# One of six GpSimd products per job goes to VectorE in two scan layers of a four-layer stack

## The chip, the cores and the metric

The kernel runs on one core of a Trainium2 chip, in one launch. The metric is device time in microseconds (us), the median of three runs. A core has five engines with queues of their own: TensorE (PE; its weight loads appear as PEld), VectorE (DVE), ScalarE (ACT), GpSimd (POOL) and SyncE (SP), which here issues nearly all transfers (DMA). An engine works off its queue strictly in order, and waits for others through semaphores.

## The reference, cut to what matters

The input x is eight images of 192 channels and 56 x 56 pixels, in float32. Four layers follow, each `x = x + layer(group_norm(x))`. Layer 0 is an involution. Layers 1, 2 and 3 are Mamba blocks: projections, a causal convolution over four positions, silu, and a selective scan along the 3136 pixels. The scan is what the change touches:

```
dbl = xc @ xproj.T                    # dt's low rank part, B and C, 16 states each
dt  = softplus(dbl[dt] @ dtproj.T + bias)
h   = h * exp(dt * A) + (dt * xc) * B     # for each of 16 states and each inner channel
y   = sum over states of h * C
out = ((y + xc * D) * silu(z)) @ out_w.T
```

Layer 1 runs three mambas of 512 inner channels on slices of 64 channels; layers 2 and 3 run one each with 384 inner channels.

## The kernel before

**Chunks and jobs.** An image is cut into 7 chunks of T = 448 pixels, so a layer has 56 chunks. A job is one mamba on one chunk: 168 jobs in layer 1, 56 in layer 2 and 56 in layer 3. The inner channels of a job come in nd groups of 128 (nd = 4 in layer 1, 3 in layers 2 and 3).

**Units.** The 16 states of a group are taken in q = 0 to 3 quarters. A unit is one group and one quarter: 32 channels x 4 states on the 128 partitions, four rows r of 448 pixels each, 1792 elements per partition. A job has nd x 4 units, so 12 in layers 2 and 3, numbered m = 0 to 11 with q = m % 4. A unit passes these stages:

- `inputs_begin` (L737): ScalarE copies the carried state into the tile uhg (9 buffers).
- the product (dt * xc) * B into uhg. Two engines can make it. GpSimd (`inputs_by_pool`, L748) reads B from `rows[0, q]`, an SBUF tile that a transfer has spread over the partitions (`row_in`, L629, rows<-bc). VectorE (`inputs_by_vector`, L754) reads B from a PSUM bank, b, which TensorE has filled by a small matmul (`spread_b`, L723). There is one such bank.
- `decays` (L729): ScalarE writes exp(dt * A) into one of two PSUM banks, da, two rows in each.
- `scan` (L758): VectorE runs the recurrence, two scans per unit, h = 0 and h = 1, each over one da bank.
- `keep` (L762): ScalarE copies the last column out as carry.
- `readout` (L767): GpSimd multiplies by C.
- `reduce` (L776): TensorE sums the states into the bank y; at q = 0 it first puts xc * D there (L773). After the last quarter of a group `gated` (L792) multiplies with silu(z) on VectorE.

**The order of the work** is written out by hand in the loop over the units (L847 and on). At step k, with m = k % 12, it issues in this order: gated, if q = 3; reduce(k-3); the first half of the background steps; scan(k, 0); decays(k+1, 0); inputs_begin(k+3); inputs_by_pool(k+2); readout(k-2); inputs_by_vector(k+1); spread_b(k+2); the second half of the background steps; scan(k, 1); keep(k); decays(k+1, 1). The set `pool_units` (L699) says which units GpSimd multiplies; spread_b and inputs_by_vector leave these out, inputs_by_pool leaves out the others. `pool_rows` is the set of q that occur in it: only for these is the row of B transferred, at m = 8 + q of the job before. So a product by GpSimd is issued two steps ahead of its scan, and one by VectorE one step ahead, between the two scans of the unit before.

**The background** is the next job's preparation, planned into two places per step (`places`, with the stretches of `bounds`): convolutions up to m = 3; at m = 4 the silu block, in which ScalarE changes its table, makes silu of xc and of z (L596, L577) and changes back (L569), then the output projection of the job before (L1129, added by L1135 on VectorE) and x_proj (L601, evicted by L605 and L606); at m = 5 and 6 the remainder of B (L612, L613, evicted by L617) and the deltas (L635, evicted by L640); at m = 7 the softplus block (L643); then the products dt * xc (L650), the stores (ops<-dt), the loads of the operands (rep<-ops, L713) and the gates. All background matmuls share two PSUM banks, mm: a third one waits until ScalarE or VectorE has evicted the first. `nothing` (L782) issues matmuls that add zero. In layer 2 a chunk also ends with batch-norm statistics on VectorE (L298), and every seventh chunk with the group norm of a whole image.

Of the kernel before, what the change touches and what calls it, by code (L numbers as in the profile page):

```python
# [86 lines left out]
def conv_mamba_stack(ctx: ExitStack, tc: tile.TileContext, a, out):  # L87
# [604 lines left out]
    def ssm_layer(pool, w, jobs, n_slots):  # L692


        nd = w.nd
        units = [(i, j, q) for i in range(len(jobs)) for j in range(nd) for q in range(NQ)]
        groups = [(i, j) for i in range(len(jobs)) for j in range(nd)]
        per_job = nd * NQ
        pool_units = {1, 3, 5, 7, 9, 11, 13, 15} if nd == 4 else {1, 3, 6, 7, 9, 11}  # L699
        pool_rows = sorted({m % NQ for m in pool_units})  # L700
        us = [Layer() for _ in jobs]
        carry = []
# [449 lines left out]
    for layer, w in enumerate((w1, w2, w3), 1):  # L1152
        with ExitStack() as stack:
            scan_banks(stack)
            pool = stack.enter_context(tc.tile_pool(name=f"ssm{layer}", bufs=1))
            load_weights(pool, w)
            with tc.manual_schedule():
                if layer == 1:
                    ssm_layer(pool, w, mamba_jobs(pool, w), 3)
                else:  # L1160
                    ssm_layer(pool, w, dense_jobs(pool, w, layer), 1)
# [69 lines left out]
```

## Time and profile before

| what | before |
|---|---|
| median of three runs | 25285.75 us (25262.34 to 25312.53) |
| the profiled execution: time, span | 25314.83 us, 25313.0 us |
| mean granted TensorE clock | 0.827 of full speed |
| layer 2, from its first matmul L1082 to that of layer 3 | 17417 to 21390 us |
| layer 3, to the end of the span | 21390 to 25313 us |
| scans L758 (VectorE) | 8064 x 2011 ns |
| readouts L767 (GpSimd) | 4032 x 3675 ns |
| products by GpSimd, L748 | 2016 x 3987 ns |
| products by VectorE, L754 | 2016 x 2000 ns |
| rows of B spread by TensorE, L723 | 2016 x 406 ns |

The durations of neighbours on one engine overlap by some hundredths of a microsecond in the profile, so a sum goes better by the distance from one start to the next: 1.92 to 1.95 us for a scan, 3.65 for a readout, 3.96 for a product by GpSimd, 1.91 to 1.93 for one by VectorE. In a line of the timeline the first two numbers are the start in us from the span's beginning and the duration in us (of all, where "x3" says that three were merged); in brackets stands how long the engine was idle before it, and what released it. In a row of the table by stretch each engine has its busy time and its number of instructions; behind them come the granted clock, the share of the DMA engines and GB/s.

### The profile page before, as it was taken

To read this page: it belongs to the slowest core of one execution; us is meant where nothing else is said; L and a number is where in the kernel's file an instruction comes from. 1 tells how busy PE (TensorE), PEld (TensorE's weight loads), DVE (VectorE), ACT (ScalarE), POOL (GpSimd) and SP (SyncE) were. 2 spreads that over 40 slices of the span, in tenths; PEclk is the share of its full clock that TensorE was granted. 3 is DMA by queue.
4 is the path that set the end of the run, shared out by engine and by line. 5 is a ranking of instruction groups with operands and counts; after the bars stand their busy time and mean duration, and the time that the engine had idled before them with its cause. 6 is when DMAs were issued, how large, how long until landed. Compare 5 with 4: busy or idle time off the path is not lost.

```text
span 25313.0 us, 232064 instructions
## 1 busy us (share of the span) xinstructions
PE 21123.4 (83%) x71870; PEld 6720.0 (27%) x71870; DVE 22641.3 (89%) x15661; ACT 16946.5 (67%) x32354; POOL 23383.1 (92%) x6772
## 2 busy tenths in 40 slices
PE   9988888888888888888888888888888887888888
PEld 3322222222222222222222222222333332333332
DVE  8879988998899889998998899897999998999998
ACT  1137776767766776766776676676777776777776
POOL 4469999999999999999999999998999998999999
PEclk9988777877777777777777787778888888888888
DMA  4433333333333333333333333333444443444443
GB/s 106 105 101 123 122 119 117 122 121 119 118 122 121 119 120 119 123 119 119 123 119 120 121 120 118 121 119 108 139 141 136 139 140 120 141 138 139 138 145 128
DMA packets 1184872, 3132.61 MB, mean 124 GB/s; under 512 B 163756, under 2 KB 446404, under 8 KB 1183496
## 3 DMA queue, kind: packets, MB, share of 16 engines
q1 hardware_dynamic: 1180824, 3116.70, 37.9%
q8 instruction: 564, 9.24, 0.1%
q14 instruction: 684, 5.60, 0.1%
q10 hardware_dynamic: 2800, 1.06, 0.0%
HBM read 2399.92 MB, written 555.55 MB: 117 GB/s over the span
## 4 chain that ended last, share of the span: by engine, by line
DVE 29%; PE 25%; ACT 19%; issue 11%; POOL 9%; DMA 6%; SPq 2%; DVEq 0%; POOLq 0%; ACTq 0%
DVE uhg L758 20%; ACT da L729 8%; DVE uhg L754 6%; POOL uhg L767 6%; PE y L776 4%; PE mm L635 4%; POOL uhg L748 3%; PE mm L416 3%; DMA rows<-bc 3%; PE y L782 2%; ACT L569 2%; PE y_inv L451 2%; PE y L773 2%; PE mm L612 2%; DMA rep<-ops 2%
## 5 line engine op out<-in xcount | busy, mean ns | idle before, releaser
L758 DVE TENSOR_TENSOR_SCAN uhg<-da,uhg 128x898 f32<-128x898 f32 x8064 | 15928.1, 2011 | 1284.0 <-ACT da L729 1261.9
L767 POOL TENSOR_TENSOR uhg<-uhg,rows 128x1792 f32<-128x1792 f32 x4032 | 14746.3, 3675 | 654.5 <-ACT carry L762 425.9
L729 ACT ACTIVATE da<-rep,k 128x448 f32<-128x448 f32 x16128 | 10255.9, 636 | 1816.6 <-DVE uhg L758 1438.7
L748 POOL TENSOR_TENSOR uhg<-rep,rows 128x1792 f32<-128x1792 f32 x2016 | 8038.2, 3987 | 375.5 <-DMA rep<-ops 206.2
L776 PE MATMUL y<-uhg,k 128*32 128x448 f32 x32256 | 4756.8, 666 | 562.0 <-POOL uhg L767 560.2
L754 DVE TENSOR_TENSOR uhg<-rep,b 128x1792 f32<-128x1792 f32 x2016 | 4031.8, 2000 | 658.9 <-PE b L723 615.1
L762 ACT COPY carry<-uhg 128x4 f32<-128x4 f32 x4032 | 787.3, 195 | 3514.0 <-DVE uhg L758 3464.3
L773 PE MATMUL y<-xc,w_d 128*128 128x448 f32 x2016 | 1522.0, 850 | 1580.5 <-DVE zs L792 1580.3
L782 PE MATMUL y<-w_d,k 128*128 128x448 f32 (+1 forms) x5166 | 2465.1, 586 | 0.0
L1026 PE MATMUL mm<-xs,k 128*128 128x448 f32 x2688 | 1289.7, 617 | 479.6 <-DMA xs<-xg 318.7
L776 PEld LDWEIGHTS y<-uhg,k 128*32 128x32 f32 x32256 | 695.1, 117 | 3664.1 <-issue 2204.0
L1082 PE MATMUL mm<-v,w_in 96*128 96x448 f32 x2688 | 1427.9, 662 | 199.7 <-ACT zs L676 92.4
L635 PE MATMUL mm<-dbl,w_dt 36*128 36x448 f32 (+1 forms) x2016 | 1469.0, 840 | 127.0 <-ACT k L617 127.0
L782 PEld LDWEIGHTS y<-w_d,k 128*128 128x128 f32 x5166 | 1035.4, 215 | 1486.5 <-issue 1459.8
L436 POOL TENSOR_TENSOR x<-x,one 96x448 f32<-96x448 f32 x560 | 633.3, 1135 | 668.3 <-DVE one L428 650.7
L612 PE MATMUL mm<-dbl,k 16*16 16x448 f32 x1120 | 692.7, 707 | 515.7 <-ACT dbl L605 515.7
L428 DVE TENSOR_TENSOR prod<-mm,shifted 128x448 f32<-128x448 f32 x1680 | 932.6, 609 | 207.8 <-PE mm L416 187.3
L1109 PE MATMUL mm<-xin,w_conv 128*128 128x448 f32 x2688 | 1076.4, 543 | 2.0 <-ACT xin L674 1.0
L773 PEld LDWEIGHTS y<-xc,w_d 128*128 128x128 f32 x2016 | 455.0, 265 | 2191.9 <-DVE zs L792 1509.5
L647 PE MATMUL mm<-xc,k 128*128 128x448 f32 x2016 | 983.7, 599 | 31.1 <-DVE dt L650 30.3
L723 PE MATMUL b<-k,k 96*128 96x448 bf16 x2016 | 819.1, 406 | 129.9 <-DVE uhg L754 129.8
L593 ACT ACTIVATE xc<-mm,k 128x448 f32<-128x448 f32 x1008 | 615.3, 627 | 438.9 <-PE mm L1026 327.1
(134 smaller groups left out, 19720.0 us busy)
## 6 DMA issues: line engine op xcount, KB each, us to landing
rep<-ops SPq DMA_DIRECT2D x4032, 448.0 KB, 5.7
ops<-dt SPq DMA_DIRECT2D x1008, 448.0 KB, 3.3
rows<-bc SPq DMA_DIRECT2D x1792, 224.0 KB, 6.2
shifted<-xpad SPq DMA_DIRECT2D x672, 179.0 KB, 4.6
xg<-stream SPq DMA_DIRECT2D x168, 336.0 KB, 3.7
xr<-stream SPq DMA_DIRECT2D x168, 336.0 KB, 5.3
stream<-xr SPq DMA_DIRECT2D x112, 336.0 KB, 3.2
xs<-xg SPq DMA_DIRECT2D x224, 112.0 KB, 6.1
```

The lines of the kernel that those rows point to most:

```text
L612: nc.tensor.matmul(u.left[m][:NS, :T], lhsT=ident[:NS, :NS], rhs=u.dbl[:NS, :], start=True, stop=False)
L635: nc.tensor.matmul(u.dps[j][:, :T], lhsT=w.dtw[:, j * 128 : (j + 1) * 128], rhs=u.dbl[:nk, :], start=True, stop=True)
L729: nc.scalar.activation(t[:, 64 + 449 * r : 512 + 449 * r], reps[k // NQ][:, 2 * h + r, 0, :], AF.Exp, scale=w.neg_a[:, j * NR + 2 * h + r, ...
L748: nc.gpsimd.tensor_mul(uhg[k][:, :, 1:], reps[k // NQ][:, :, 1, :], b)
L754: nc.vector.tensor_mul(uhg[k][:, :, 1:], reps[k // NQ][:, :, 1, :], b)
L758: nc.vector.tensor_tensor_scan(v, banks.da[h][:, 63:961], v, 0.0, ALU.mult, ALU.add)
L767: nc.gpsimd.tensor_mul(v, v, us[i].rows[1, q].unsqueeze(1).to_broadcast([128, NR, T]))
L773: nc.tensor.matmul(ys[k // NQ][:, :T], lhsT=w.dd[:, j, :], rhs=us[i].xc[:, j, :], start=True, stop=False)
L776: nc.tensor.matmul(y[32 * r : 32 * r + 32, :T], lhsT=fold, rhs=uhg[k][:, r, 1:], start=False, stop=(q == NQ - 1))
L782: nc.tensor.matmul(ys[k // NQ][:, : nd * 112], lhsT=zeros, rhs=w.dd.rearrange("p j e -> p (j e)")[:, : nd * 112], start=False, stop=False,)
L1026: nc.tensor.matmul(pm[:, :T], lhsT=w.inconv[:, k, j * 128 : (j + 1) * 128], rhs=ck.xs[:, i, 2 - 2 * k : 2 - 2 * k + T], start=(k == 0), st ...
L1082: nc.tensor.matmul(pm[:, :T], lhsT=w.inw[:, k, m * 128 : (m + 1) * 128], rhs=ck.v[:, k, :], start=(k == 0), stop=(k == NCT - 1),)
```

## The change

For jobs of 12 units, which are those of layers 2 and 3, unit 6 leaves the set of GpSimd's units:

```diff
-        pool_units = {1, 3, 5, 7, 9, 11, 13, 15} if nd == 4 else {1, 3, 6, 7, 9, 11}
+        pool_units = {1, 3, 5, 7, 9, 11, 13, 15} if nd == 4 else {1, 3, 7, 9, 11}
```

In a job VectorE's products were those of units 0, 2, 4, 5, 8 and 10; unit 6 joins them, so that 4, 5 and 6 stand in a row. Its product is no longer issued on GpSimd's queue at step 4 but on VectorE's at step 5, between the two scans of unit 5; spread_b is issued for it at step 4. `pool_rows` becomes {1, 3} instead of {1, 2, 3}, so the transfer of the row of B for q = 2 at m = 10 falls away. The tile tag of these rows keeps its four buffers. Layers 0 and 1 are issued as before.

## The prediction

> **What bounds the kernel now.** I read the busy line of the page first, then the table by stretch over the steady parts of layers 2 and 3 (the only ones whose set of units changes), and then the timelines of single jobs.
>
> ```profile
> PE 21123.4 (83%) x71870; PEld 6720.0 (27%) x71870; DVE 22641.3 (89%) x15661; ACT 16946.5 (67%) x32354; POOL 23383.1 (92%) x6772
> ```
> ```profile
> 17600.00:21300.00 3700.00, 3138.96 (x11083) 1130.85 (x11083) 3412.05 (x2176) 2736.07 (x5215) 3576.50 (x964) 0.89 0.42 138
> 21600.00:25250.00 3650.00, 3192.75 (x11025) 1128.75 (x11024) 3320.54 (x2016) 2708.14 (x5186) 3572.55 (x963) 0.88 0.42 140
> ```
>
> The columns are PE, PEld, DVE, ACT, POOL, then the granted clock. GpSimd is busy 97% and 98% of these stretches, VectorE 92% and 91%. That looks like a GpSimd bound, but the jobs speak against it. I took the distance from the first scan of a job to the first scan of the next. In layer 2 it is 68.24 us in 38 of 55 cases, within 0.02 us; seven are 75 to 79 (the end of an image, with its group norm) and nine average 70.1; the mean is 69.6. In those equal jobs GpSimd's idle time varies from 0 to 6.2 us and the readout of unit 0 trails its scan by 1.5 to 8.7 us, yet the period does not move. So GpSimd does not set it. VectorE's idle hardly varies, 4.8 to 5.0 us a job, always in the same four places: ahead of the first scans of units 1, 5, 7 and 8 (1.33, 1.72, 1.01, 0.89), each ended by ScalarE's decays. Layer 2 goes by a ring of VectorE and ScalarE. The part that matters, on VectorE, from the second scan of unit 4 to the first of unit 7:
>
> ```profile
> 18743.63 2.02 DVE L758 TENSOR_TENSOR_SCAN uhg<-da,uhg 128x898 f32<-128x898 f32 x1
> 18745.57 0.59 DVE L1135 TENSOR_TENSOR xr<-xr,mm 96x448 f32<-96x448 f32 x1
> 18747.88 2.03 DVE L758 TENSOR_TENSOR_SCAN uhg<-da,uhg 128x898 f32<-128x898 f32 x1 [1.72 <-ACT da L729]
> 18749.83 0.59 DVE L1135 TENSOR_TENSOR xr<-xr,mm 96x448 f32<-96x448 f32 x1
> 18750.34 5.85 DVE L758 TENSOR_TENSOR_SCAN uhg<-da,uhg 128x898 f32<-128x898 f32 x3
> 18756.11 0.59 DVE L792 TENSOR_TENSOR zs<-zs,y 128x448 f32<-128x448 f32 x1
> 18757.71 2.03 DVE L758 TENSOR_TENSOR_SCAN uhg<-da,uhg 128x898 f32<-128x898 f32 x1 [1.01 <-ACT da L729]
> ```
>
> and on ScalarE, from the carry of unit 5 to the decays of unit 7, with TensorE's two groups between:
>
> ```profile
> 18752.39 0.20 ACT L762 COPY carry<-uhg 128x4 f32<-128x4 f32 x1 [0.17 <-DVE uhg L758]
> 18752.49 1.30 ACT L729 ACTIVATE da<-rep,k 128x448 f32<-128x448 f32 x2
> 18753.82 0.52 ACT L617 CAST k<-mm 16x448 bf16<-16x448 f32 x1
> 18754.36 0.64 ACT L640 ACTIVATE dt<-mm,k 128x448 f32<-128x448 f32 x1
> 18755.77 0.63 ACT L640 ACTIVATE dt<-mm,k 128x448 f32<-128x448 f32 x1 [0.78 <-PE mm L635]
> 18756.31 1.30 ACT L729 ACTIVATE da<-rep,k 128x448 f32<-128x448 f32 x2
> ```
> ```profile
> 18753.83 0.96 PE L776 MATMUL y<-uhg,k 128*32 128x448 f32 x8
> 18754.72 1.02 PE L635 MATMUL mm<-dbl,w_dt 44*128 44x448 f32 x2
> ```
>
> Read it as a chain: the second scan of unit 5 ends (18752.28), ScalarE's carry, the second decays of unit 6, the eviction L617, which frees one of the two mm banks for TensorE's L635, then L640, then the first decays of unit 7, then VectorE may scan. VectorE's own way (two scans, L792) is 1.01 us shorter.
>
> Layer 3 has no batch-norm statistics. Twelve of its 55 distances are 67.0 to 67.1 us, with the same four waits; that is its undisturbed period, 67.02. But the mean is 68.78: 17 are 68.36, and 25 average 69.9. In nearly all of the long ones a stretch of half clock lies on the deltas: in one at 23415 to 23425 the granted clock is 0.50, L635 x2 takes 1.86 instead of 1.02, and the wait ahead of unit 7 is 2.76 instead of 1.01. In the 68.36 jobs a short slow stretch lies on the convolutions. In layer 2's equal jobs the slow stretch always falls some 54 to 68 us into the job, where it costs nothing.
>
> **The change part by part.** Per job, in 112 jobs.
>
> GpSimd loses one L748: 3.96 us from its start to the next instruction's. A job needs 12 x 3.65 + 6 x 3.96 = 67.6 us of GpSimd, then 63.6. Layer 2 shows what that is worth: nothing, since a changing lag leaves the period alone. The one place where GpSimd does end the work is the drain of each layer, five readouts in a row; the last scan of layer 3 ends at 25294.2 and the last readout at 25301.3. There GpSimd comes up to 3.96 earlier while VectorE's scans come up to 1.93 later: I take 2 us gained per layer, 4 in all (bounds 0 and 8).
>
> SP loses one row transfer per job (rows<-bc, 224 KB), since no unit with remainder 2 is left with GpSimd. GpSimd's first product of a job already waits for such a transfer (70.5 us in 36 waits in the layer 2 stretch) without moving the period: 0, from 0 to a little gained.
>
> TensorE gains one L723 of 0.35 us. It must wait until VectorE has read the row of unit 5 out of the only b bank, which ends at 18743.7, and it stands ahead of the output projection (L1129, begun at 18743.01). So L1129, L601 and L605 move by about 1.1 us. L1129's first half then ends near 18746.5, and the addition L1135 ahead of unit 5's scan still fits into its 1.72 us of idle. L601 would end near 18751.2, when ScalarE comes to L605 (18751.27). Cost 0. The cover is thin: at half clock, up to about 1 us in such a job.
>
> VectorE gains one L754, 1.93 us from start to next start. In program order it stands after the first scan of unit 5 and ahead of L1135 and of that unit's second scan. All that follows begins 1.93 later: the second scan, hence carry, decays of unit 6 and L617. The 1.01 us of idle ahead of unit 7 does not hide it, because the idle ends at the end of a chain that begins at this very scan. One thing is given back: L617 ended about 18754.3, but TensorE was in L776 until 18754.7 and only then began L635. With L617 at about 18756.2 TensorE is free, so L635 starts about 0.3 sooner after it. Shift: 1.93 - 0.28 = 1.65 us per job. Bounds: 0, if all four waits could hide it, and 1.93.
>
> The dearest unknown is TensorE's clock, since the job's length and TensorE's pauses both change. Before, its price is 1.76 us a job in layer 3 (68.78 - 67.02) and about 0 in the equal jobs of layer 2. For each layer after it I bound the price by 0 and 1.76. For layer 2 I keep what there is. For layer 3, whose new undisturbed period of 68.67 comes near layer 2's old one, I take half, 0.88.
>
> What sets a slow stretch off can be seen once: TensorE waits for a readout, and the clock is low after it.
>
> ```profile
> 18773.71 1.72 PE L776 MATMUL y<-uhg,k 128*32 128x448 f32 x8 [4.05 <-POOL uhg L767]
> ```
> ```profile
> 18772.00:18786.00 14.00, 10.17 (x25) 3.08 (x26) 14.00 (x9) 7.47 (x16) 12.75 (x4) 0.53 0.70 255
> ```
>
> [...]
>
> [...]
>
> **The sum.** Layer 2: 56 x 1.65 = 92. Layer 3: 56 x (1.65 - 0.88) = 43. Drains: -4. Together 131 us on the profiled 25314.83. That execution is 0.1% above the median of the runs shown, 25285.75; I add the 131 to the median: **25417 us**.
>
> **The rivals.**
> 1. The clock gets worse: with periods off 68.24 layer 2 loses its harmless slot and pays 1.76, layer 3 keeps its 1.76. 92 + 92 + 99 - 4 = 279: 25565. For it: layer 3's scatter. Against: a longer job leaves TensorE more room.
> 2. The product is partly hidden, say a shift of 0.8 us, as much as the smallest of the four waits: 112 x 0.8 - 56 x 0.88 - 4 = 36: 25322, no change to be told.
> 3. Faster: GpSimd is the bound after all, and layer 3's scatter and layer 2's nine jobs of 70.1 come from its lag through TensorE's readout sums (L776 waits for L767, 645 us in PE and PEld together in layer 3's stretch). Then 56 x 1.76 + 9 x 1.86 = 115 go, and with the product lying in the waits around units 5 and 7 the time is 25286 - 115 - 4 = 25167. It turns to the slow side from a shift of 119/112 = 1.06 us per job. Against: 1.01 is all the idle there, and it moves with the scan.
> 4. The edit does nothing at run time: 25286. The sets of units feed spread_b, both input functions and the row loads alike, so I hardly believe it.
>
> **How the numbers follow.** Forecast 0.58, clock worse 0.18, partly hidden 0.16, faster 0.06, nothing 0.02. The forecast's own range is 82 to 180 (layer 3's clock price 0 or whole): 25368 to 25466. The range of 8 in 10 takes in the partly hidden case and most of the worse clock: 25315 to 25540. A measurement here can tell about 0.2%, 51 us. Slower by more: 0.58 + 0.18 = 0.76; within: 0.18; faster: 0.06.
>
> **What the profile after would show.** L748 1904 times and L754 2128 times. VectorE's scans of units 5 and 6 no longer three in a row after L1135, but a product ahead of it. The equal period of layer 2 at 69.9, the wait ahead of unit 7 near 0.7, the others unmoved; GpSimd 89 to 92% busy in both stretches, with its added idle ahead of a readout or a row transfer. I am wrong if layer 2's commonest period is below 69.3 (the chain does not begin at unit 5's scan), or if layer 3's least period falls below 67.0 (then GpSimd did bind it).

## The result, and the profile after

The changed kernel takes **25569.79 us** (median of four runs, 25557.68 to 25585.67), against 25287.67 for the kernel before in the same runs (25262.34 to 25312.53): a ratio of 1.0112, 95% interval [1.0094, 1.0129]. It is slower, as forecast, but by 282 us in place of 131, and outside the range. The time is that of rival 1, though only in part by the way that rival 1 gave.

The page after, busy times first, then the two groups of products:

```profile
PE 21286.5 (83%) x71982; PEld 6758.0 (26%) x71982; DVE 22861.9 (89%) x15773; ACT 16949.1 (66%) x32354; POOL 22947.4 (90%) x6660
...
L748 POOL TENSOR_TENSOR uhg<-rep,rows 128x1792 f32<-128x1792 f32 x1904 | 7590.8, 3987 | 724.1 <-DMA rows<-bc 477.1
L754 DVE TENSOR_TENSOR uhg<-rep,b 128x1792 f32<-128x1792 f32 x2128 | 4253.4, 1999 | 676.7 <-PE b L723 633.9
```

The counts are as forecast (1904 and 2128): 112 products went over. GpSimd has 436 us less to do and nothing came of it. The table by stretch over the steady parts of layers 2 and 3 (PE, PEld, DVE, ACT, POOL, granted clock):

```profile
17600.00:21300.00 3700.00, 3138.74 (x10650) 1109.37 (x10646) 3352.19 (x2132) 2618.62 (x4981) 3220.21 (x871) 0.85 0.39 129
21700.00:25350.00 3650.00, 3132.89 (x10739) 1105.35 (x10736) 3322.97 (x2005) 2623.28 (x5023) 3257.96 (x881) 0.86 0.40 132
```

GpSimd went from 97 and 98% to 87 and 89% (89 to 92 was forecast). VectorE has one product more per job and is not busier: 91% in both. So the jobs grew by more than the product. And the granted clock fell from 0.89 and 0.88 to 0.85 and 0.86.

The time by jobs (distance from the first scan of a job to the next, 55 distances per layer):

| | before | after | grown by |
|---|---|---|---|
| layer 2, mean; commonest; least | 69.59; 68.24; 68.23 | 72.81; 72.03; 71.38 | 177 us in 55 |
| layer 3, mean; commonest; least | 68.78; 68.36; 67.01 | 71.04; 70.79; 69.76 | 124 us in 55 |

Layers 0 and 1 are the same in both. The first matmul of layer 2 comes 22 us earlier after (17394.7 against 17416.8), which is scatter: over the fourteen kernels of this document the first scan of layer 2 starts anywhere from 17431 to 17468. So the whole of it lies in the two layers, spread over all jobs. VectorE from the end of the second scan of unit 4 on, in a job with the commonest distance (the 32nd of layer 2, begun at 19705.97):

```profile
19733.75 0.62 DVE L1135 TENSOR_TENSOR xr<-xr,mm 96x448 f32<-96x448 f32 x1 [0.76 <-PE mm L1129]
19735.22 2.03 DVE L758 TENSOR_TENSOR_SCAN uhg<-da,uhg 128x898 f32<-128x898 f32 x1 [0.85 <-ACT da L729]
19737.17 1.99 DVE L754 TENSOR_TENSOR uhg<-rep,b 128x1792 f32<-128x1792 f32 x1
19739.08 0.61 DVE L1135 TENSOR_TENSOR xr<-xr,mm 96x448 f32<-96x448 f32 x1
19739.61 5.85 DVE L758 TENSOR_TENSOR_SCAN uhg<-da,uhg 128x898 f32<-128x898 f32 x3
19745.38 0.59 DVE L792 TENSOR_TENSOR zs<-zs,y 128x448 f32<-128x448 f32 x1
19747.50 2.03 DVE L758 TENSOR_TENSOR_SCAN uhg<-da,uhg 128x898 f32<-128x898 f32 x1 [1.52 <-ACT da L729]
19749.90 2.02 DVE L754 TENSOR_TENSOR uhg<-rep,b 128x1792 f32<-128x1792 f32 x1 [0.38 <-PE b L723]
```

The new L754 stands where the forecast put it. Before unit 5 the wait for L1129 (0.76) has taken the place of half of the old 1.72: the late output projection is hidden, as forecast. But the wait ahead of unit 7 is 1.52, where 0.7 was forecast, and the product of unit 8 now waits 0.38 for its row of B, which it did not before. ScalarE and TensorE in the same job:

```profile
19741.66 0.20 ACT L762 COPY carry<-uhg 128x4 f32<-128x4 f32 x1 [2.11 <-DVE uhg L758]
19741.76 1.30 ACT L729 ACTIVATE da<-rep,k 128x448 f32<-128x448 f32 x2
19743.09 0.52 ACT L617 CAST k<-mm 16x448 bf16<-16x448 f32 x1
```
```profile
19739.83 0.91 PE L612 MATMUL mm<-dbl,k 16*16 16x448 f32 x2 [0.59 <-DVE xr L1135]
...
19740.86 1.02 PE L635 MATMUL mm<-dbl,w_dt 44*128 44x448 f32 x2
19741.81 0.96 PE L776 MATMUL y<-uhg,k 128*32 128x448 f32 x8
19743.67 1.86 PE L635 MATMUL mm<-dbl,w_dt 44*128 44x448 f32 x2 [0.90 <-ACT k L617]
19745.45 1.67 PE L612 MATMUL mm<-dbl,k 16*16 16x448 f32 x2
```

Carry and L617 are late by the new product. TensorE, which before went from L776 straight into L635, now pauses 0.90 for the bank; in layer 2 it does so 53 times, 43.6 us in all. (The 0.59 ahead of the first L612 is not new: in the prediction's job TensorE waited 0.81 there, for L605.) Behind the pause the same L635 takes 1.86 instead of 1.02 and L612 1.67 instead of 0.91: **half clock**. The table by stretch, cut at like parts of a job, shows it. First the kernel before, in the job of the prediction's timelines, then the one after (the granted clock stands behind the five engines):

```profile
18754.62:18765.62 11.00, 9.83 (x41) 3.37 (x38) 9.11 (x8) 10.02 (x18) 11.00 (x4) 1.00 0.07 26
18765.62:18772.62 7.00, 4.03 (x18) 1.55 (x16) 7.00 (x6) 4.01 (x9) 7.00 (x3) 1.00 0.68 194
18772.62:18786.86 14.24, 11.03 (x27) 3.44 (x28) 14.24 (x9) 7.47 (x16) 12.99 (x5) 0.52 0.71 253
```
```profile
19741.97:19752.97 11.00, 10.10 (x27) 2.09 (x19) 9.10 (x6) 8.14 (x15) 7.53 (x3) 0.54 0.00 1
19752.97:19765.97 13.00, 11.24 (x51) 4.51 (x48) 11.46 (x11) 9.12 (x17) 12.15 (x4) 1.00 0.61 205
19765.97:19778.00 12.03, 6.01 (x16) 1.95 (x16) 12.03 (x9) 6.08 (x13) 9.05 (x3) 0.57 0.55 204
```

Before, the only slow stretch of this job lay at its end, where VectorE was busy throughout (14.24 of 14.24), so it cost nothing. After, a second one lies 36 to 47 us into the job, on the deltas and the matmuls behind them, whose results VectorE waits for. What that does to VectorE over the whole of layer 2 (busy, mean ns, then idle ahead of the group), before and after:

```profile
L758 DVE TENSOR_TENSOR_SCAN uhg<-da,uhg 128x898 f32<-128x898 f32 x1344 | 2663.6, 2012 | 276.2 <-ACT da L729 271.3 <-POOL uhg L767 4.4 <-DVE uhg L754 0.5
L754 DVE TENSOR_TENSOR uhg<-rep,b 128x1792 f32<-128x1792 f32 x335 | 668.6, 1996 | 8.2 <-PE b L723 8.2
L650 DVE TENSOR_TENSOR dt<-dt,mm 128x448 f32<-128x448 f32 x165 | 95.4, 603 | 4.0 <-PE mm L647 3.6 <-ACT dt L643 0.2
L1135 DVE TENSOR_TENSOR xr<-xr,mm 96x448 f32<-96x448 f32 x110 | 65.1, 593 | 0.0
```
```profile
L758 DVE TENSOR_TENSOR_SCAN uhg<-da,uhg 128x898 f32<-128x898 f32 x1344 | 2663.0, 2011 | 246.3 <-ACT da L729 243.1 <-POOL uhg L767 2.6 <-DVE uhg L754 0.5
L754 DVE TENSOR_TENSOR uhg<-rep,b 128x1792 f32<-128x1792 f32 x391 | 781.7, 1999 | 39.9 <-PE b L723 39.9
L650 DVE TENSOR_TENSOR dt<-dt,mm 128x448 f32<-128x448 f32 x165 | 100.4, 612 | 29.5 <-PE mm L647 23.6 <-ACT dt L643 3.1
L1135 DVE TENSOR_TENSOR xr<-xr,mm 96x448 f32<-96x448 f32 x110 | 67.4, 613 | 41.1 <-PE mm L1129 41.1
```

The products cost 113 us more (56 of 2.0). Of the scans' idle only 30 us went, although the product covers about 1 us ahead of unit 5 in each job, since part came back ahead of unit 7. And 98 us of new waits for TensorE stand in three places (31.7, 25.5 and 41.1).

### The profile page after: what moved, and what is told of

Its sections match the earlier page's. It is cut to its first block, busy times and chain, and to the rows that moved or that the text cites. A ratio compares the mean times of both kernels' runs of the same rounds, so it can differ in the third digit from the quotient of the medians.

```text
span 25583.5 us, 231744 instructions
## 1 busy us (share of the span) xinstructions
PE 21286.5 (83%) x71982; PEld 6758.0 (26%) x71982; DVE 22861.9 (89%) x15773; ACT 16949.1 (66%) x32354; POOL 22947.4 (90%) x6660
## 4 chain that ended last, share of the span: by engine, by line
DVE 32%; PE 26%; ACT 20%; issue 10%; DMA 5%; POOL 5%; SPq 1%; DVEq 0%; POOLq 0%; ACTq 0%
DVE uhg L758 22%; ACT da L729 8%; DVE uhg L754 7%; PE mm L635 5%; PE y L776 4%; POOL uhg L767 3%; PE mm L416 3%; DMA rows<-bc 2%; PE y L782 2%; ACT L569 2%; PE mm L612 2%; PE y L773 2%; PE y_inv L451 2%; POOL uhg L748 2%; ACT zs L577 2%
## 5 line engine op out<-in xcount | busy, mean ns | idle before, releaser
L767 POOL TENSOR_TENSOR uhg<-uhg,rows 128x1792 f32<-128x1792 f32 x4032 | 14745.2, 3674 | 1012.7 <-ACT carry L762 788.6
L748 POOL TENSOR_TENSOR uhg<-rep,rows 128x1792 f32<-128x1792 f32 x1904 | 7590.8, 3987 | 724.1 <-DMA rows<-bc 477.1
L754 DVE TENSOR_TENSOR uhg<-rep,b 128x1792 f32<-128x1792 f32 x2128 | 4253.4, 1999 | 676.7 <-PE b L723 633.9
L776 PE MATMUL y<-uhg,k 128*32 128x448 f32 x32256 | 4753.0, 665 | 68.0 <-POOL uhg L767 66.1
L773 PE MATMUL y<-xc,w_d 128*128 128x448 f32 x2016 | 1582.5, 882 | 1992.6 <-DVE zs L792 1992.4
L635 PE MATMUL mm<-dbl,w_dt 36*128 36x448 f32 (+1 forms) x2016 | 1575.6, 896 | 207.2 <-ACT k L617 206.3
L776 PEld LDWEIGHTS y<-uhg,k 128*32 128x32 f32 x32256 | 695.4, 117 | 3209.2 <-issue 2360.6
L1082 PE MATMUL mm<-v,w_in 96*128 96x448 f32 x2688 | 1321.7, 619 | 204.0 <-ACT zs L676 98.2
L773 PEld LDWEIGHTS y<-xc,w_d 128*128 128x128 f32 x2016 | 472.8, 274 | 2674.5 <-DVE zs L792 1986.6
L612 PE MATMUL mm<-dbl,k 16*16 16x448 f32 x1120 | 744.8, 756 | 503.5 <-ACT dbl L605 459.8
```

What stands on the lines that cost most here:

```text
L612: nc.tensor.matmul(u.left[m][:NS, :T], lhsT=ident[:NS, :NS], rhs=u.dbl[:NS, :], start=True, stop=False)
L635: nc.tensor.matmul(u.dps[j][:, :T], lhsT=w.dtw[:, j * 128 : (j + 1) * 128], rhs=u.dbl[:nk, :], start=True, stop=True)
L748: nc.gpsimd.tensor_mul(uhg[k][:, :, 1:], reps[k // NQ][:, :, 1, :], b)
L754: nc.vector.tensor_mul(uhg[k][:, :, 1:], reps[k // NQ][:, :, 1, :], b)
L767: nc.gpsimd.tensor_mul(v, v, us[i].rows[1, q].unsqueeze(1).to_broadcast([128, NR, T]))
L773: nc.tensor.matmul(ys[k // NQ][:, :T], lhsT=w.dd[:, j, :], rhs=us[i].xc[:, j, :], start=True, stop=False)
```

## The experiments

**The theories.** (A) The new product delays carry and L617; TensorE, which at that point has only small matmuls, pauses for the bank; its clock goes to half on the deltas, and this doubles the price. (B) The price is VectorE's longer work, the product plus waits that follow from it, and the clock only goes along with the longer job. (C) It comes from GpSimd's changed load, or from the row transfer that fell away. (D) It is the single b bank, which delays L1129, a cover that I had called thin.

The measure that separates them is read from the clock records of each trace. In those of the two kernels TensorE's clock is full or half, and it changes after whole multiples of 3.413 us (1657 of 1658 stretches before, 1825 of 1826 after); such a length is called a slot below. The measure is how many of the 12 us from 36 to 48 us of a job are at half clock, on average over the 55 jobs that have a distance. Beside it stand the start of L617 in layer 2's jobs (the second of the three in a job; median, from the job's first scan), the mean distances of layers 2 and 3, and the time against the kernel before, which was timed beside each group of experiments (medians 25304.45 beside e1 to e4, 25290.9 beside e5 to e8, 25306.21 beside e9 to e12).

| kernel | L617 at | half clock, 36 to 48: layer 2; 3 | mean distance: layer 2; 3 | us, ratio to before, interval |
|---|---|---|---|---|
| before | 35.2 | 0.9; 4.6 | 69.59; 68.78 | |
| after | 37.1 | 9.5; 9.4 | 72.81; 71.04 | 25569.79, 1.0112 [1.0094, 1.0129] |
| e1 after, 3 zero groups | 38.4 | 1.1; 0.7 | 72.02; 70.18 | 25485.37, 1.0075 [1.0063, 1.0088] |
| e2 after, product earlier | 35.3 | 1.9; 3.1 | 69.59; 68.30 | 25266.81, 0.9984 [0.9975, 0.9993] |
| e3 unit 7 in place of 6 | 35.2 | 3.2; 4.1 | 69.55; 68.36 | 25254.19, 0.9983 [0.9975, 0.9992] |
| e4 before, less GpSimd | 35.2 | 0.7; 2.7 | 69.13; 68.53 | 25274.73, 0.9988 [0.9979, 0.9997] |
| e5 after, L617 first | 35.0 | 5.0; 3.7 | 70.57; 69.10 | 25363.83, 1.0027 [1.0018, 1.0036] |
| e6 after, 3 weak groups | 38.4 | 10.0; 9.9 | 74.69; 72.05 | 25740.72, 1.0179 [1.0165, 1.0193] |
| e7 before, L617 delayed | 37.0 | 9.9; 10.1 | 72.98; 70.98 | 25599.69, 1.0120 [1.0106, 1.0134] |
| e8 after, GpSimd as before | 37.1 | 9.9; 9.4 | 72.90; 71.08 | 25584.43, 1.0113 [1.0099, 1.0127] |
| e9 before, L617 first | 34.4 | 0.6; 4.0 | 69.49; 68.84 | 25305.3, 1.0002 [0.9993, 1.0011] |
| e10 as e2, L617 first | 34.5 | 1.9; 1.7 | 69.50; 68.17 | 25263.44, 0.9989 [0.9981, 0.9998] |
| e11 as e3, L617 first | 34.4 | 2.6; 4.5 | 69.35; 68.40 | 25259.56, 0.9982 [0.9974, 0.9991] |
| e12 after, 2 zero groups | 37.1 | 1.9; 1.6 | 71.22; 69.28 | 25385.63, 1.0041 [1.0029, 1.0054] |

**e1_warm_deltas** fills TensorE's pauses with matmuls that add zero, one behind the sums of unit 2 and two ahead of those of unit 3:

```diff
+            if nd == 3 and m == 6:
+                nothing(k - 4, 2)
             if k >= 3:
                 reduce(k - 3)
+            if nd == 3 and m == 5:
+                nothing(k - 3, 1)
```

> The changed kernel with three more zero-adding matmuls per job in layers 2 and 3, one behind the readout sum of step 5 and two ahead of that of step 6, in TensorE's pauses ahead of the deltas. Clock theory (the later L617 leaves TensorE so little used ahead of the deltas that its clock is halved just on them): the half clock leaves the deltas, layer 2's commonest period falls from 72.0 to 69.9 to 70.3 us, the time from 25570 to 25330 to 25440. Length theory (the job is longer by the product, and the clock is low wherever a longer job puts it): no change, 25540 to 25600. GpSimd theory (a GpSimd that is ahead has moved TensorE's pauses): the pauses elsewhere stay, 25500 to 25600.

The half clock left the deltas and the ratio fell from 1.0112 to 1.0075, less than expected. Undisturbed jobs took 70.3 and 69.1, 0.4 more than the forecast's 69.89 and 68.67, since two groups are longer than the pause and push L635 back; and in about half of the jobs of layer 2 a half-clock slot now fell on the convolutions, 4 to 8 us into the job, which costs some 1.7 us there. The clock carries at least a part of the price; a better fitting filler was wanted (e12).

**e2_early_product** issues the product of unit 6 behind the second scan of unit 4 instead of between the scans of unit 5:

```diff
-            if k + 1 < n_units:
+            if k + 1 < n_units and not (nd == 3 and m == 5):
                 inputs_by_vector(k + 1)
...
                 decays(k + 1, 1)
+            if nd == 3 and m == 4:
+                inputs_by_vector(k + 2)
```

> The changed kernel with VectorE's product of unit 6 issued half a step earlier, behind the second scan of unit 4 and ahead of the first of unit 5, where VectorE waits 1.72 us for the silu block. Clock theory with the chain as forecast: the product is hidden but for 0.2 us, L617 comes no later, the half clock does not lie on the deltas: 25230 to 25340. Length theory: VectorE has the same work, 25500 to 25600. GpSimd theory: 1.65 us per job less, the clock as in the changed kernel, 25370 to 25420.

Met, at the good end. There the product lies in the wait ahead of unit 5, which falls from 1.67 to 0.00; carry and L617 are as early as before, and the whole price is gone. It has as many products on VectorE, the same load on GpSimd and as many rows through the b bank as the changed kernel. So neither VectorE's added work (B) nor GpSimd (C) nor the bank (D) has a price of its own; the place of the product has.

**e3_unit_7** lets VectorE take unit 7 in place of 6, that is `pool_units` = {1, 3, 6, 9, 11}.

> VectorE takes the product of unit 7 in place of that of unit 6, so GpSimd keeps 1, 3, 6, 9, 11. It stands between the two scans of unit 6, behind the start of the chain to L617. Clock theory: 1.0 of its 1.93 us lies in the wait ahead of unit 7, L617 is not delayed: 25330 to 25420, and no more half clock on the deltas than before. Length theory and GpSimd theory: one product more on VectorE and one less on GpSimd as in the change, 25500 to 25600.

Missed to the good side: nothing is paid. Its product stands between the scans of unit 6, behind carry and L617 of the chain, and fills the waits ahead of units 7 and 8 (means 1.09 and 0.87, now 0.05 and 0.09). VectorE in a job of layer 2:

```profile
17759.09 1.99 DVE L754 TENSOR_TENSOR uhg<-rep,b 128x1792 f32<-128x1792 f32 x1
17761.01 2.02 DVE L758 TENSOR_TENSOR_SCAN uhg<-da,uhg 128x898 f32<-128x898 f32 x1
...
17763.46 2.01 DVE L758 TENSOR_TENSOR_SCAN uhg<-da,uhg 128x898 f32<-128x898 f32 x1
```

No wait is left ahead of unit 7's scan at 17763.46, and it starts 39.9 us into the job instead of 39.1, which the next wait gives back: the distance stays 68.24.

**e4_gpsimd_less** takes work from GpSimd and gives it to nobody: in the kernel before, zeros are written for unit 6 in place of its product, and the row for q = 2 is not transferred.

```diff
-        pool_rows = sorted({m % NQ for m in pool_units})
+        pool_rows = sorted({m % NQ for m in pool_units if nd == 4 or m != 6})
...
+            if nd == 3 and k % per_job == 6:
+                nc.gpsimd.memset(uhg[k][:, :, 1:], 0.0)
+                return
```

> The kernel before, with GpSimd's product of unit 6 left out: GpSimd fills the tile with zeros instead, and the row transfer for q = 2 is gone; VectorE does nothing more. Clock theory: GpSimd is not what bounds and L617 is not moved, 25220 to 25340. GpSimd theory: TensorE's clock falls on the deltas as in the changed kernel, without the shift, 25370 to 25420. If GpSimd were the bound after all: 25120 to 25200.

Met: 0.12% faster, and layer 2's commonest distance is 68.24 as before. Writing the zeros takes 1.60 us where the product took 3.99, so GpSimd has 269 us less to do in all. A lighter GpSimd is worth next to nothing here, which rules out rival 3.

**e5_after_evict** keeps the product where the change put it, and issues L617 ahead of the carry of unit 5:

```diff
             bg.run(plan[2 * m + 1])
+            if nd == 3 and m == 5:
+                bg.flush(1)
             nothing(k - 3, more > 1)
```

> The changed kernel with one order undone on ScalarE: in layers 2 and 3 the copy of k (L617) is issued ahead of the carry of unit 5, so that it no longer waits behind a carry that now ends later. Chain theory with the clock (the late copy leaves TensorE idle 0.9 us ahead of L635, that tips a slot under the bound, and the deltas run at half clock): the half clock leaves the stretch 36 to 48 us of the job in most jobs, the wait ahead of unit 7 falls from 1.5 to under 0.8 us, undisturbed jobs take 69.0 to 69.9 (layer 2) and 67.8 to 68.7 (layer 3), time 25300 to 25420. Theory that VectorE's longer work or GpSimd's load sets the job's length: 25540 to 25600, as the changed kernel.

The time was as expected: the ratio fell from 1.0112 to 1.0027, some 210 us, for an order of two ScalarE instructions. ScalarE in an undisturbed job:

```profile
17696.20 0.52 ACT L617 CAST k<-mm 16x448 bf16<-16x448 f32 x1 [1.41 <-PE mm L613]
17696.90 0.20 ACT L762 COPY carry<-uhg 128x4 f32<-128x4 f32 x1 [0.17 <-DVE uhg L758]
...
17698.24 1.38 ACT L640 ACTIVATE dt<-mm,k 128x448 f32<-128x448 f32 x2
```

L617 starts as soon as L613 has delivered (ScalarE had waited 1.41 for it), TensorE has its bank, and both L640 follow without a wait. The wait ahead of unit 7 fell to 0.2, and undisturbed jobs to 68.87 and 67.64: a shift of 0.63 only. The half clock left the deltas in part of the jobs alone, less than I expected: 24 jobs of 55 in layer 2 and 18 in layer 3 still have over 5 us of it there. This edit shortens the chain as well as the pause, so by itself it doesn't tell how much of the 210 us is clock.

**e6_after_weak** is e1 with the added matmuls on 16 x 16 of the array in place of 128 x 128, with the same 336 columns:

```diff
+        def weak(k, n):
+            for _ in range(n):
+                nc.tensor.matmul(
+                    ys[k // NQ][:16, : nd * 112], lhsT=zeros[:16, :16], rhs=w.dd.rearrange("p j e -> p (j e)")[:16, : nd * 112],
+                    start=False, stop=False,
+                )
```

> As e1_warm_deltas, with the three added groups of matmuls of the same columns but 16 x 16 of the array in place of the whole: TensorE is as busy in the gaps, and hardly more of its array is used. All added matmuls multiply zeros. If the clock goes by the use of the array: the half clock stays on the deltas (36 to 48 us of the job), time 25560 to 25640. If it goes by idle time: the half clock is gone there as in e1_warm_deltas, 25460 to 25520.

The half clock stayed on this part of all but two of 110 jobs. The time is worse than either theory's number, since here the groups stand ahead of the sums and push L635 back, at half clock behind them. TensorE in the third job of layer 2, in e1 and then in e6, with the table by stretch of the 3.41 us that end where e6's clock falls (17632.02):

```profile
17618.40 0.92 PE L612 MATMUL mm<-dbl,k 16*16 16x448 f32 x2
...
17619.44 1.02 PE L635 MATMUL mm<-dbl,w_dt 44*128 44x448 f32 x2
17620.39 1.40 PE L782 MATMUL y<-w_d,k 128*128 128x336 f32 x4
17621.72 0.96 PE L776 MATMUL y<-uhg,k 128*32 128x448 f32 x8
17622.61 1.02 PE L635 MATMUL mm<-dbl,w_dt 44*128 44x448 f32 x2
```
```profile
17628.69 0.91 PE L612 MATMUL mm<-dbl,k 16*16 16x448 f32 x2
...
17629.72 1.02 PE L635 MATMUL mm<-dbl,w_dt 44*128 44x448 f32 x2
17630.66 1.30 PE L789 MATMUL y<-w_d,k 16*16 16x336 f32 x4
17631.89 1.65 PE L776 MATMUL y<-uhg,k 128*32 128x448 f32 x8
17633.47 1.86 PE L635 MATMUL mm<-dbl,w_dt 44*128 44x448 f32 x2
```
```profile
17628.61:17632.02 3.41, 3.41 (x14) 1.00 0.07 17
```

The two schedules run alike up to the sums L776, with no pause in either. With the whole array the clock stays; with a corner of it the clock halves, behind 3.41 us of which TensorE was busy 3.41. So in these runs the clock did not go by idle time alone; what the two differ in is how much of the array the added matmuls use.

**e7_before_late** moves no product. It delays L617 in the kernel before by two ScalarE copies:

```diff
+            if nd == 3 and m == 6:
+                for _ in range(2):
+                    nc.scalar.copy(late, w.convd.rearrange("p j k e -> p (j k e)")[:, : 2 * T])
```

> The kernel before, no product moved, with two ScalarE copies of 896 elements (some 1.9 us) added in layers 2 and 3 ahead of the copy of k (L617), which delays it about as the change does. Chain theory with the clock: the delay alone brings the half clock to the deltas, 25480 to 25600, with the stretch 36 to 48 us of layer 2's jobs mostly at half clock. Theory that the added work on VectorE makes the job longer: 25270 to 25340, as before.

25599.69, the top of what theory A expected, and the half clock lies on the deltas as in the changed kernel. ScalarE in a job of layer 2:

```profile
17709.77 0.20 ACT L762 COPY carry<-uhg 128x4 f32<-128x4 f32 x1 [0.18 <-DVE uhg L758]
...
17711.11 1.89 ACT L876 COPY late<-w_conv 128x896 f32<-128x896 f32 x2
17713.03 0.52 ACT L617 CAST k<-mm 16x448 bf16<-16x448 f32 x1
```

Of the 3.68 us by which its commonest distance grew (68.24 to 71.92), 1.82 are the delay of L617 itself (35.20 to 37.02); the rest came without any new work on VectorE. All 110 jobs have over 5 us of half clock on this part. A late L617 is enough to bring it.

**e8_after_both** lets GpSimd make the product of unit 6 in the changed kernel as well, into a tile that nobody reads, with its row transferred again.

```diff
+        def again_by_pool(k):
+            i, j, q = units[k]
+            b = us[i].rows[0, q].unsqueeze(1).to_broadcast([128, 2, T])
+            for r in (0, 2):
+                nc.gpsimd.tensor_mul(scratch, reps[k // NQ][:, r : r + 2, 1, :], b)
```

> The changed kernel with GpSimd making its old product of unit 6 as well, into a tile that nobody reads, so that GpSimd's load and its stream of rows are those of before and VectorE's load that of after. Chain theory: the length is VectorE's order and the clock alone, 25550 to 25630. If the missing GpSimd work is what moved the clock or the timing (GpSimd ahead of its buffers, other transfers): under 25500.

Met: with GpSimd's old load the changed kernel is as slow as without. Theory C is out.

**e9_before_evict**, **e10_early_evict** and **e11_unit7_evict** put the edit of e5 into the kernel before, into e2 and into e3.

> The kernel before with the edit of e5_after_evict alone: the copy of k (L617) ahead of the carry of unit 5. Chain theory: before, that copy starts at 35.2 us of the job and is behind the carry by little, so this frees at most 0.9 us per job ahead of unit 7 and VectorE is bound by its own work after that: 25190 to 25310, 68.24 for layer 2's commonest period becoming 67.4 to 68.2. If the gain of e5 over the changed kernel came from the order alone and not from the product's effect on it, this would gain as much, some 200 us: 25060 to 25110.

> e2_early_product with the edit of e5_after_evict. Chain theory: the copy of k starts at 35.3 us there, nearly where it can; up to 0.9 us per job ahead of unit 7, most of it a wait that VectorE then spends elsewhere: 25190 to 25280. If VectorE's work alone set the length, no gain over e2: 25260 to 25290.

> e3_unit_7 with the edit of e5_after_evict. There the wait ahead of unit 7 is already filled by the product (0.05 us left), so an earlier copy of k finds VectorE busy: no gain, 25230 to 25290.

None gained on the kernel that it was put into. For e11 that was expected; the time of e10 lies in the ranges of both its theories and decides nothing. In e9 the time is inside what I expected, but layer 2's commonest distance did not fall below 68.24: the wait of unit 7 shrank from 1.09 to 0.26 and 0.73 appeared ahead of the second scan of unit 6, whose decays now stand behind L617. So the order by itself gains nothing; the 210 us of e5 are there only where the product has made the carry late.

**e12_after_warm1** is e1 with one group in place of two ahead of the sums of unit 3, so that 0.73 us of zeros go into the pause of 0.90:

```diff
             if nd == 3 and m == 6:
-                nothing(k - 4, 2)
+                nothing(k - 4, 1)
```

> e1_warm_deltas with one zero group in place of two ahead of the sums of unit 3, so that the added work (0.73 us) fits into the 0.90 us in which TensorE waits for k and delays nothing. Chain theory: undisturbed jobs at the length that was forecast from the shift of 1.65 us alone, 69.8 to 70.1 (layer 2) and 68.5 to 68.8 (layer 3), the half clock off the deltas in most jobs, time 25400 to 25490 (a second stretch at 4 to 8 us of the job, as in e1, keeps it above 25417). If one group is not enough to lift the slot, the half clock stays and the time is 25540 to 25600.

It came out a little below the expected time. This is the changed kernel with its late product, its late L617 (37.1) and, in nearly all jobs, the deltas at full clock. Its TensorE and VectorE in the fifth job of layer 2, and the table by stretch over the part that was at 0.54 in the changed kernel:

```profile
17750.70 0.83 PE L782 MATMUL y<-w_d,k 128*128 128x336 f32 x2
17751.46 0.96 PE L776 MATMUL y<-uhg,k 128*32 128x448 f32 x8
17752.44 1.02 PE L635 MATMUL mm<-dbl,w_dt 44*128 44x448 f32 x2
```
```profile
17755.43 2.03 DVE L758 TENSOR_TENSOR_SCAN uhg<-da,uhg 128x898 f32<-128x898 f32 x1 [0.68 <-ACT da L729]
```
```profile
17750.74:17761.74 11.00, 9.87 (x43) 2.96 (x42) 10.32 (x8) 10.31 (x16) 9.74 (x4) 1.00 0.00 0
```

The wait ahead of unit 7 is 0.68 in this undisturbed job, and undisturbed jobs take 69.85 and 68.61. Against the undisturbed 68.24 and 67.01 of before that is a shift of 1.61 and 1.60 us per job, with no clock in it.

## Why the prediction was wrong, step by step

**The shift: right.** The forecast said 1.65 us per job for the way from the new product to unit 7's scan, with a wait of 0.7 left there and a distance of 69.9 in layer 2; e12 measures 1.61, 0.68 and 69.85. The cover over L1129 held, the four waits did not hide the product, and e2 and e3 show why: the same product placed off this chain costs nothing.

**The clock: the step that failed.** The prediction put it as "For each layer after it I bound the price by 0 and 1.76", kept layer 2 free of it ("For layer 2 I keep what there is") and gave back half in layer 3. With the undisturbed jobs of e12 as the base, the commonest job after stands 2.18 above in layer 2 (72.03 against 69.85) and in layer 3 (70.79 against 68.61), and all 110 jobs have at least 6.8 us of half clock between 34 and 50 us. Before, 1.76 was layer 3's mean and layer 2's commonest job paid nothing. So both prices are beyond the bound. In sums over the 55 distances of each layer, with e12 as the changed kernel without half clock on the deltas:

| | layer 2 | layer 3 | together | forecast, per 56 jobs |
|---|---|---|---|---|
| e12 less before | 90 | 28 | 118 | 92 + 43 = 135 |
| after less e12 | 88 | 97 | 184 | 0 |
| after less before | 177 | 124 | 302 | 135 |

The first line is close to the forecast, 118 for 135, and the second is what it lacked. (The sums are rounded, and the split is an estimate, as e12 also differs in where its other slow stretches fall. In layer 3, 28 for 43, its zeros also take away half clock that was there before: the mean lay 1.76 above an undisturbed job before, and lies 0.67 above one in e12.) The error was in the bound: 1.76 is a mean over layer 3's jobs, of which 30 of 55 had no half clock, or little, on the deltas. The prediction's own rows had the price of a job that has it: 25 jobs averaged 69.9 against 67.02, some 2.9 us. As the share of affected jobs can go to one, the bound was 2.9 and not 1.76. And it had the cause in its own working: it computed that L617 would end when TensorE had long left L776 (18756.2 against 18754.7), used this to subtract 0.28, and did not ask what a pause of TensorE at its least used place would do to the clock.

Layer 2's freedom from it, which the prediction kept, hung on its period, as an estimate from the clock records: 20 slots of 3.413 us are 68.27, so at 68.24 a slow stretch falls on the same harmless place job after job (measured, it begins 53.8 to 55.1 us into each of the 38 equal jobs). Five jobs of layer 2 lay otherwise before and had half clock on the deltas; they averaged 70.1.

**Rival 1** had the time (25565) and named the term. Its cause, "periods off 68.24", is a part of the truth and not the main one. In e5, where L617 is as early as before and the period 68.87, layer 2 has half clock on the deltas in 24 of 55 jobs, against 5 before; so losing the place costs something. But with the late L617 it is 110 of 110 jobs (after, e7, e8), wherever the slots fall, against 30 before and 42 in e5, and with zeros in the pause (e12) jobs of 69.85 keep the deltas at full clock. No run changes the period alone, so the two shares are not measured. Its "Against", that a longer job leaves TensorE more room, didn't decide. **Rival 2** (partly hidden) fails with the shift of 1.61. **Rival 3** (GpSimd is the bound) fails by e4 and e8. **The drains** came out about as forecast: the last readout ends 4.0 us behind the last scan in both layers, against 6.2 and 7.1 before, so some 5 us for 4.

**The low end of the range, 82**, stood for a layer 3 whose clock price goes to 0. The slow stretch that the prediction shows stood with TensorE's wait of 4.05 us for GpSimd. Such waits did go (in the steady part of layer 2 L776 waited 227.5 us for L767 before, 5.6 after), but TensorE then waited for VectorE (L773 for L792, 285.4 us against 117.2), and the slow stretch at the end of the job stayed (0.57 in the rows above).

**The slow stretches.** The one on the deltas in the job shown lasts three slots, 10.24 us, from 19742.78 to 19753.02. It begins with the pause of 0.90, and in the slot ahead of it TensorE is busy for 2.93 of 3.41 us. So a pause as long as the prediction's 4.05 us was not needed here, and in e6 the clock fell behind a slot with no pause.

## What to carry to other kernels

A piece of work added to an engine with idle time is free only if it stands in a wait that does not itself hang on what the work delays: the same 1.9 us cost 282 us between the scans of unit 5, and nothing ahead of unit 5 (e2) or behind the first scan of unit 6 (e3), both some 0.16% faster than the kernel before. When a price depends on a state (here half clock), bound it by the price of one affected job times all jobs, not by today's mean. And look at TensorE's clock where it works through narrow matmuls (16 and 44 rows here) with short pauses: around the pauses of 0.59 and 0.90 us the deltas of all 110 jobs of the changed kernel had half clock, and a filler that fits the pause and uses the whole array kept them at full clock in nearly all jobs (e12), one on 16 x 16 of it in two of 110 (e6). Compare the job's period with the slots too: before, where layer 2's commonest is 68.24, near 20 of them, five of its 55 jobs had over 5 us of half clock on the deltas, and in e5, with 68.87 in undisturbed jobs, 24 did, though no run changed the period alone.

## What the runs showed of the hardware

In e6 TensorE's clock was halved at 17632.02, behind 3.41 us of which it was busy for 3.41, with the added matmuls on 16 x 16 of the array; in e1, with 128 x 128 in the same places, the L635 behind them kept its 1.02 us. Busy time alone tells the slots apart badly: in the kernel before, of the slots of layers 2 and 3 at full clock that kept it 430 of 1565 had TensorE busy for less than 90% of the time, and in e6 the clock fell behind 106 slots, of 270, in which it was busy for 95% or more.

The use of the array is an estimate of mine from the shapes and times in the traces: each matmul's time at full clock (0.37 us for 448 columns in float32, by the distance from one start to the next) is weighted by the rows x columns that it uses, as a share of the 128 x 128 of the largest, and summed over a slot. In the kernel before, the slots that kept the full clock have a median of 0.73, those behind which it fell one of 0.20. In the cases shown, the slot ahead of the half clock in the changed kernel's job has 0.30, e6's has 0.12, and the slots of e1 around its deltas 0.33 to 0.78. The two kinds overlap, so no bound is read from this, nor did a run measure the one of which the expectation of e5 speaks; whether the rows or the columns count was not tried.
